# First linear map of 28 chunks by seven half-size products instead of eight

## The chip, the cores and the metric

The kernel runs on one core of one Trainium2 chip. A core has TensorE (PE, with its weight loads listed apart as PEld), VectorE (DVE), ScalarE (ACT), GpSimd (POOL) and SyncE (SP, which only issues DMAs here), each with its own in-order queue. They share the on-chip memory SBUF; TensorE writes its results to eight PSUM banks of 128 x 512 fp32, from which VectorE and ScalarE read. The metric is device time in microseconds (us) from start to end; lower is better. "The span" is the time from the first to the last instruction in one profiled execution.

## The reference

Two layers, all in fp32, on x of 8 batches x 2048 nodes x 256 features:

```python
A_norm = A + eye(n);  deg = A_norm.sum(0) + A_norm.sum(1) - diagonal(A_norm)
A_hat = A_norm * rsqrt(deg)[:, None] * rsqrt(deg)[None, :]
agg = einsum('nm,bmd->bnd', A_hat, features)            # 2048 x 2048 per batch
h   = relu(batchnorm(agg.reshape(-1, 256) @ W1.T + b1)) # first linear map, 256 -> 512
out = batchnorm(h @ W2.T + b2)                          # second linear map, 512 -> 256
x = layernorm(x + out)                                  # layer 0
x = layernorm(x + masked_attention(x, W, adj))          # layer 1, 4 heads, adj == 0 masked
```

The two batch norms take their mean and variance over all 8 x 2048 rows, so every row of h has to exist before the first relu. The change lies in `agg @ W1.T + b1`.

## The kernel before

**Stages.** (1) The adjacency matrix is loaded, transposed on TensorE into eight quarter tiles, and the degrees are summed. (2) The aggregation and the first linear map, which this document is about. (3) The last four chunks of the first linear map, then batch norm, relu and the second linear map, with h read back from HBM. (4) Attention, the longest stage.

**The aggregation** runs over 16 units `(k, b, d)`: k (0 or 1) picks two chunks of 512 output nodes, b a pair of batches, d a half (128) of the features. One unit is itself done by a seven-product scheme (Strassen-Winograd): seven products p1 to p7 instead of eight, each eight fp32 matmuls of 128x128 by 128x512 into one PSUM bank (pool `psa`, four banks). Its stationary operands are the forms `S` of x: four loaded tiles, scaled by `dinv` on GpSimd (`scale`, L303), and their sums and differences `s1` to `s4` (L316 to L328, GpSimd). Its moving operands are the quarters `T` of the adjacency matrix and their forms `t1` to `t4` (VectorE, 128x4096 elements each, L429 and L341 to L349). The products leave PSUM by one ScalarE copy (L394) and seven VectorE additions into the four tiles `ag[i, j]` (i the batch of the pair, j the chunk), each of which GpSimd then multiplies by `dbc` (L414, L436, L446, L452: c11, c21, c22, c12, in this order). The next unit's x tiles are loaded by SP (L168) after p1, scaled after p2, and s1 to s4 made behind p7 and p4. A tile name of x is reused when its product is done.

**The turn.** After unit 7 k goes from 0 to 1, and all quarters T are replaced within unit 7: SP fetches them (L353), VectorE makes a mask and t1 to t4.

**Masks.** Attention needs `adj == 0` as bytes. `mask_of` (L185) makes a quarter's mask on VectorE and SP stores it; three per k, in units 1, 2 and 3 of each k (and one at the turn).

**The first linear map.** After each odd unit (d = 1) both feature halves of four chunks are there (two batches, two chunks each), and `linear` runs for each of the four: for each of four output blocks of 128, two accumulating matmuls into a bank of `psh` (three banks), a ScalarE eviction that adds b1 (L370), VectorE `bn_stats` of the result (L371), and after the four an SP store of h to HBM (L372). That is 8 matmuls for each chunk. It is done for 7 of the 8 pairs of units, 28 chunks; the last four chunks (L588) stay on chip and are not touched by the change.

**The order of the work** on every engine in stages 2 and 3 is the order in which the code is written (`manual_schedule`), and an engine that waits holds up all that is behind it in its queue. A tile of a pool with one buffer is rewritten only when its readers are done.

**The second linear map** (L538 to L581) already works by seven products of half size: GpSimd makes the forms of h (`form`, L538, 128x1024 elements), TensorE runs each product as two matmuls into a bank (L543), ScalarE copies the first product (L551), VectorE adds the rest (L569, L570, L577, and L560 where the bias is added), and `bn_stats` follow (L557).

## Time and profile before

| what | us |
|---|---|
| median of three runs (3593.39 to 3596.04) | 3595.87 |
| the profiled execution, its own time | 3594.16 |
| its span | 3592.4 |
| TensorE busy in the span | 3545.7 (99%) |
| VectorE, ScalarE, GpSimd busy | 1989.2, 1637.4, 2265.2 |
| first-map matmuls L366 (448 records), busy | 193.4 |
| aggregation matmuls L333 (1792 records), busy | 772.1 |
| mean granted TensorE clock | 0.996 |

Every fp32 matmul of this size leaves two records in the profile: 28 chunks x 8 matmuls are the 448 records of L366. Matmuls overlap in their pipeline, so a record's duration (592 ns) is longer than the distance to the next one. In a row of the timeline the columns are start and length in us, engine, line, operation, output<-input, shape, and count of the merged instructions; in brackets stand the engine's idle time before it and what ended that.

### The profile page before, as it was taken

What the parts mean: (1) busy time and instruction counts of PE and PEld (TensorE: products, weight loads), DVE (VectorE), ACT (ScalarE), POOL (GpSimd) and SP (SyncE); (2) the same over time, 40 slices, a digit from 0 to 9 for tenths busy, and PEclk for the clock granted to TensorE, in tenths of its full rate; (3) what the DMA queues carried; (4) which work ended last, traced back from release to release, by engine and by line L of the source; (5) the groups of instructions that cost most, each with busy time, mean ns of one, the idle gap of its engine ahead of it and who ended that gap; (6) DMA issues with size and microseconds to landing.
All of it is one profiled execution on the core that took longest, in us unless ns stands there. A gap on an engine that the chain in (4) does not pass through costs nothing. (4 is left out here: it accounts for less than half of the span.)

```text
span 3592.4 us, 55051 instructions
## 1 busy us (share of the span) xinstructions
PE 3545.7 (99%) x22503; PEld 1470.5 (41%) x22503; DVE 1989.2 (55%) x2929; ACT 1637.4 (46%) x2036; POOL 2265.2 (63%) x1530
## 2 busy tenths in 40 slices
PE   8999999999999999999999999999999999999997
PEld 5444444444444443343433343433343334343332
DVE  6212141220146656766766776676676676667666
ACT  5101100110135455655665665565566566566555
POOL 3543263434237647777777777777777777777777
PEclk9999999999999999999999999999999999999999
DMA  9222232221247445666566566556566556555555
GB/s 339 68 73 88 82 135 82 76 84 45 82 167 274 160 88 101 123 136 122 114 138 121 118 136 130 112 125 140 112 124 134 118 114 147 115 115 118 118 112 114
DMA packets 197142, 440.14 MB, mean 123 GB/s; under 512 B 14080, under 2 KB 121104, under 8 KB 186384
## 3 DMA queue, kind: packets, MB, share of 16 engines
q0 software_dynamic: 64656, 239.37, 35.1%
q1 hardware_dynamic: 132048, 196.11, 15.9%
q8 instruction: 178, 2.92, 0.3%
q10 hardware_dynamic: 176, 1.06, 0.1%
q14 instruction: 84, 0.69, 0.1%
HBM read 126.62 MB, written 75.51 MB: 56 GB/s over the span
## 5 line engine op out<-in xcount | busy, mean ns | idle before, releaser
L860 ACT ACTIVATE prob<-prob 128x1024 f32<-128x1024 f32 x1024 | 1081.2, 1056 | 913.1 <-DVE prob L854 836.8
L854 DVE SCALAR_TENSOR_TENSOR prob<-mask,st 128x1024 f32<-128x1024 uint8 x1024 | 1239.1, 1215 | 434.4 <-PE st L842 358.4
L872 PE MATMUL out_ps<-prob,v 64*64 64x512 f32 x8192 | 1074.2, 595 | 3.6 <-DVE ot L898 2.6
L842 PE MATMUL st<-qt,kt 64*64 64x512 f32 x8192 | 1062.8, 589 | 0.1
L893 POOL TENSOR_TENSOR acc<-acc,prob 128x1024 f32<-128x1024 f32 x319 | 829.4, 2600 | 7.7 <-DMA prob<-prob 2.7
L333 PE MATMUL pa<-t,x 128*128 128x512 f32 x1792 | 772.1, 593 | 2.7 <-ACT x L309 2.7
L882 POOL DMA_DIRECT2D prob<-prob x447 | 403.8, 929 | 566.2 <-PE out_ps L872 456.0
L842 PEld LDWEIGHTS st<-qt,kt 64*64 64x64 f32 x8192 | 312.5, 133 | 566.7 <-issue 526.4
L333 PEld LDWEIGHTS pa<-t,x 128*128 128x128 f32 x1792 | 341.0, 190 | 431.8 <-issue 427.8
L872 PEld LDWEIGHTS out_ps<-prob,v 64*64 64x64 f32 x8192 | 290.7, 133 | 542.4 <-issue 468.0
L414 POOL TENSOR_TENSOR ag<-ag,dbc 128x512 f32<-128x512 f32 x16 | 20.2, 1264 | 484.9 <-DVE ag L413 452.3
L884 POOL TENSOR_TENSOR acc<-acc,prob 128x1024 f32<-128x1024 f32 x126 | 298.1, 2366 | 7.5
L370 ACT ACTIVATE h<-ph,b1s 128x512 f32<-128x512 f32 x112 | 76.9, 687 | 404.4 <-PE ph L366 404.4
L777 PE MATMUL pm<-x1t,wq 128*128 128x512 f32 x512 | 250.8, 613 | 0.7 <-ACT x1t L746 0.7
L394 ACT COPY ag<-pa 128x512 f32<-128x512 f32 x16 | 9.4, 586 | 421.5 <-PE pa L333 408.2
L366 PE MATMUL ph<-ag,w1s 128*128 128x512 f32 x448 | 193.4, 592 | 0.0
L891 POOL TENSOR_TENSOR acc<-prob 128x1024 f32<-128x1024 f32 x64 | 171.1, 2673 | 1.7 <-DMA prob<-prob 1.7
L672 ACT ACTIVATE x<-x,ln_nm,ln_rs 128x256 f32<-128x256 f32 x256 | 137.5, 586 | 10.5 <-POOL ln_nm L668 10.5
L777 PEld LDWEIGHTS pm<-x1t,wq 128*128 128x128 f32 x512 | 86.9, 189 | 118.3 <-issue 111.6
L944 DVE SCALAR_TENSOR_TENSOR x<-pm,ri,x 128x64 f32<-128x64 f32 x512 | 109.5, 276 | 43.8 <-PE pm L936 43.8
L371 DVE BATCH_NORM_STATS2 st<-h 128x6 f32<-128x512 f32 x112 | 76.8, 692 | 99.1 <-ACT h L370 99.1
L366 PEld LDWEIGHTS ph<-ag,w1s 128*128 128x128 f32 x448 | 85.1, 190 | 107.1 <-issue 106.9
(139 smaller groups left out, 2614.3 us busy)
## 6 DMA issues: line engine op xcount, KB each, us to landing
prob<-prob POOLq DMA_DIRECT2D x447, 512.0 KB, 4.9
x<-in_x_dram SPq DMA_DIRECT2D x92, 512.0 KB, 5.3
h_d<-h SPq DMA_DIRECT2D x28, 1024.0 KB, 3.9
t<-h_d SPq DMA_DIRECT2D x28, 1024.0 KB, 8.4
a<-in_adj_dram SPq DMA_DIRECT2D x16, 1024.0 KB, 5.0
y_d<-ag SPq DMA_DIRECT2D x32, 512.0 KB, 2.6
out_dram<-x SPq DMA_DIRECT2D x31, 512.0 KB, 6.5
yt<-y_d SPq DMA_DIRECT2D x28, 512.0 KB, 3.2
```

The source lines that it names most:

```text
L333: nc.tensor.matmul(pa, s.t[:, m, :], t[:, m, :], start=(m == 0), stop=(m == HT - 1))
L366: nc.tensor.matmul(ph, w1s[:, d, f * P : (f + 1) * P], ag[:, d, :], start=(d == 0), stop=(d == ND - 1),)
L672: nc.scalar.activation(self.t[:, i, :], self.t[:, i, :], AF.Identity, bias=self.nm[:, i : i + 1], scale=self.rs[:, i : i + 1],)
L777: nc.tensor.matmul(pm, wq[:, d, wcols], xt[:, d, cols], start=(d == 0), stop=(d == ND - 1))
L842: nc.tensor.matmul(st[r * HD : (r + 1) * HD, h, :], kt[hs, j * P + r * HD : j * P + (r + 1) * HD], qt[hs, cols], start=True, stop=True,)
L854: nc.vector.scalar_tensor_tensor(p, mask[:, j, cols][:, None, :].to_broadcast([P, 2, CH]), MASKED, st, op0=ALU.mult, op1=ALU.add,)
L860: nc.scalar.activation(probs[g], probs[g], AF.Exp)
L872: nc.tensor.matmul(outs[u][hs, r, :], inp.qkv[b, hp][2][rs, j, hs], probs[g][rs, h, :], start=(j == 0), stop=(j == NT - 1),)
L882: nc.gpsimd.dma_start(probs[g - 1], probs[g], accum_op=ALU.add)
L884: nc.gpsimd.tensor_add(accs[u], accs[u], probs[g])
L891: nc.gpsimd.tensor_add(accs[v], probs[g - 7], probs[g - 5])
L893: nc.gpsimd.tensor_add(accs[v], accs[v], probs[g - 5])
```

## The change

The first linear map of a batch i is now done for its two chunks together, by the same kind of seven-product scheme. W1 is cut in four blocks of 128 inputs x 256 outputs, the four tiles `ag[i, c][:, j, :]` (feature half j, chunk c) are the blocks of the other factor, and each of the seven products is a 128-deep product with 256 outputs: two matmuls, each alone in a PSUM bank. So 14 matmuls take the place of 16 for a batch, 28 of 32 for a pair of units.

- **Forms of W1** (`w1f`): four 128x256 additions on GpSimd, once, ahead of the first unit.
- **Forms of ag** (`linear_form`): four 128x512 subtractions on GpSimd for each batch; form 1 ahead of p7 of the odd unit, form 2 in a new tile `g2`, forms 3 and 4 within `linear`, written over operands that a product has just read.
- **Evictions**: ScalarE copies the first product (two banks); VectorE takes the twelve other banks with 14 instructions (additions, and additions with b1), and the eight `bn_stats` come at the end of `linear`.
- **Place**: `linear` of batch 1 stands where the map stood. `linear` of batch 0 is put off (`later`) to the next unit, between its p1 and p6, with its two stores of h ahead of that unit's loads of x in SP's queue.
- **At the turn** t4 (VectorE), s1 and s2 (GpSimd) of the next unit move behind `linear` of batch 1, and s3 and s4 behind that of batch 0; before, all stood in unit 7 ahead of the map.
- **Masks** move from units 1, 2, 3 of each k to units 2, 4, 6.
- `dbc` holds the two chunks of one k and is loaded again (two DMAs from ScalarE's queue) at the turn; `psh` has four banks; x of batch 0 for stage 4 is loaded into `h1`, `dbc` and `w1f`.

```diff
-        def linear(n, k, b, ag, j):
-            c = b * NCH + j * NK + k
-            h = hs[n % 2] = lp.tile([P, NH, CH], F32, name=f"h{n % 2}") if n > 1 else hs[n]
-            for f in range(NH):
-                ph = psh.tile([P, CH], F32, name="ph")
-                for d in range(ND):
-                    nc.tensor.matmul(
-                        ph, w1s[:, d, f * P : (f + 1) * P], ag[:, d, :],
-                        start=(d == 0), stop=(d == ND - 1),
-                    )
-                nc.scalar.activation(h[:, f, :], ph, AF.Identity, bias=b1s[:, f : f + 1])
-                nc.vector.bn_stats(st1[:, f, c, :], h[:, f, :])
-            nc.sync.dma_start(h_d[c], h)
+        def linear_form(ag, i, n):
+            b11, b12, b21, b22 = (ag[i, c][:, j, :] for j in range(2) for c in range(2))
...
+            x, y = {
+                1: lambda: (b12, b11),
+                2: lambda: (b22, G[i, 1]),
+                3: lambda: (G[i, 2], b11),
+                4: lambda: (b21, G[i, 2]),
+            }[n]()
+            nc.gpsimd.tensor_sub(G[i, n], x, y)
+
+        def linear(k, b, ag, i):
+            cs = [(b + i) * NCH + j * NK + k for j in range(2)]
+            lo, hi = (lp.tile([P, NH, CH], F32, name=f"h{j}") for j in range(2))
+            def products(w, t):
+                for s in range(2):
+                    ph = psh.tile([P, CH], F32, name="ph")
+                    nc.tensor.matmul(ph, W1[w][:, s * P : (s + 1) * P], t, start=True, stop=True)
+                    yield s, ph
...
+            for s, p in products((0, 0), ag[i, 0][:, 0, :]):
+                nc.scalar.copy(lo[:, 2 + s, :], p)
+            linear_form(ag, i, 3)
+            for s, p in products((0, 1), ag[i, 0][:, 1, :]):
+                plus(lo, s, p, lo[:, 2 + s, :])
+            linear_form(ag, i, 4)
+            for s, p in products(2, G[i, 2]):
+                nc.vector.tensor_add(hi[:, s, :], p, lo[:, 2 + s, :])
+            for s, p in products(3, G[i, 3]):
+                nc.vector.tensor_add(hi[:, 2 + s, :], p, hi[:, s, :])
+            for s, p in products((1, 1), G[i, 4]):
+                plus(lo, 2 + s, p, hi[:, 2 + s, :])
+            nc.sync.dma_start(h_d[cs[0]], lo)
+            for s, p in products(1, G[i, 1]):
+                plus(hi, 2 + s, p, hi[:, 2 + s, :])
+                nc.vector.tensor_add(hi[:, s, :], p, hi[:, s, :])
+            for s, p in products(4, ag[i, 1][:, 1, :]):
+                plus(hi, s, p, hi[:, s, :])
+            nc.sync.dma_start(h_d[cs[1]], hi)
+            for c, h in zip(cs, (lo, hi)):
+                for f in range(NH):
+                    nc.vector.bn_stats(st1[:, f, c, :], h[:, f, :])
...
+        nc.gpsimd.tensor_add(W1[1], W1[1, 0], W1[1, 1])
+        nc.gpsimd.tensor_sub(W1[2], W1[1], W1[0, 0])
+        nc.gpsimd.tensor_sub(W1[3], W1[0, 0], W1[1, 0])
+        nc.gpsimd.tensor_sub(W1[4], W1[0, 1], W1[2])
...
             p1 = product(S[v, 0, 0], T[k, (0, 0)])
+            for f in later:
+                f()
...
+            if d and not last:
+                for i in range(2):
+                    linear_form(ag, i, 1)
             p7 = product(S[v, 3], T[k, 3])
...
-            if not last:
+            if not (last or turn):
                 s1(w)
                 s2(w)
                 s3(w)
...
             nc.gpsimd.tensor_mul(c22, c22, dbc[0][:, 1, :])
+            if d and not last:
+                linear_form(ag, 1, 2)
...
-            if turn:
-                t4(k + 1, 3)
             n = v % (len(units) // NK)
-            if n in (1, 2, 3):
-                mask_of(k, ((0, 0), (1, 0), (1, 1))[n - 1])
+            if n in (2, 4, 6):
+                mask_of(k, ((0, 0), (1, 0), (1, 1))[n // 2 - 1])
...
-            if d == ND - 1:
-                for n, (i, j) in enumerate(CHUNKS):
-                    linear(v // ND * 4 + n, k, b + i, ag[i, j], j)
+            if d:
+                linear(k, b, ag, 1)
+                linear_form(ag, 0, 2)
+                if turn:
+                    t4(k + 1, 3)
+                    s1(w)
+                    s2(w)
+                later = [lambda k=k, b=b, ag=ag: linear(k, b, ag, 0)]
+                if turn:
+                    later += [lambda w=w: s3(w), lambda w=w: s4(w)]
```

More of the change, by code (lines that the diff above doesn't have):

```diff
@@ L282, in tile_gcn_then_masked_attention, with load_dbc @@
         name="psa", bufs=4, space=PSUM
-    ) as psa, tc.tile_pool(name="psh", bufs=3, space=PSUM) as psh, tc.tile_pool(
-        name="psd", bufs=1, space=PSUM
-    ) as psd, tc.manual_schedule(engines=ALL4):
-        hs = [lp.tile([P, NH, CH], F32, name=f"h{i}") for i in range(2)]
-        dbc = lp.tile([P, N], F32, name="dbc")
+    ) as psa, tc.tile_pool(name="psh", bufs=4, space=PSUM) as psh, tc.manual_schedule(engines=ALL4):
+        for j in range(2):
+            lp.tile([P, NH, CH], F32, name=f"h{j}")
+        w1f = lp.tile([P, 4, H // 2], F32, name="w1f")
+        dbc = []
+        def load_dbc(k):
+            dbc[:] = [lp.tile([P, 2, CH], F32, name="dbc")]
+            for j in range(2):
+                t0 = j * HT + k * TPC
+                nc.scalar.dma_start(
+                    dbc[0][:, j, :],
+                    dinv_d[t0 : t0 + TPC].rearrange("t p -> (t p)")[None, :].to_broadcast([P, CH]),
+                )
         def spread_dinv():
-            pd = psd.tile([NT, P], F32, name="pd")
+            pd = psh.tile([NT, P], F32, name="ph")
             nc.tensor.transpose(pd, dinv, ident)
@@ L295, in spread_dinv @@
             nc.scalar.dma_start(dinv_d, dt)
-            nc.scalar.dma_start(
-                dbc, dinv_d.rearrange("t p -> (t p)")[None, :].to_broadcast([P, N])
-            )
+            load_dbc(0)
         def scale(v, i, j, on_act=False):
@@ L353, in fetch @@
             nc.sync.dma_start(T[k, ij], bt_d[HALVES.index(ij)])
-        def half_cols(k, j):
-            c0 = (j * NK + k) * CH
-            return slice(c0, c0 + CH)
-        def linear(n, k, b, ag, j):
-            c = b * NCH + j * NK + k
-            h = hs[n % 2] = lp.tile([P, NH, CH], F32, name=f"h{n % 2}") if n > 1 else hs[n]
-            for f in range(NH):
-                ph = psh.tile([P, CH], F32, name="ph")
-                for d in range(ND):
-                    nc.tensor.matmul(
-                        ph, w1s[:, d, f * P : (f + 1) * P], ag[:, d, :],
-                        start=(d == 0), stop=(d == ND - 1),
-                    )
-                nc.scalar.activation(h[:, f, :], ph, AF.Identity, bias=b1s[:, f : f + 1])
-                nc.vector.bn_stats(st1[:, f, c, :], h[:, f, :])
-            nc.sync.dma_start(h_d[c], h)
+        W1 = {ij: w1s[:, ij[1], ij[0] * H // 2 : (ij[0] + 1) * H // 2] for ij in HALVES}
@@ new lines, in tile_gcn_then_masked_attention @@
+        W1.update({i + 1: w1f[:, i, :] for i in range(4)})
+        G = {}
+        def linear_form(ag, i, n):
+            b11, b12, b21, b22 = (ag[i, c][:, j, :] for j in range(2) for c in range(2))
+            if n == 2:
+                G[i, 2] = lp.tile([P, CH], F32, name="g2")
+            else:
+                G[i, n] = {1: b12, 3: b11, 4: b21}[n]
+            x, y = {
[5 more added lines that the diff above has]
+            nc.gpsimd.tensor_sub(G[i, n], x, y)
@@ new lines, in linear, with plus @@
+        def linear(k, b, ag, i):
[6 more added lines that the diff above has]
+                    yield s, ph
+            def plus(h, f, p, u):
+                nc.vector.scalar_tensor_tensor(
+                    h[:, f, :], p, b1s[:, f : f + 1], u, op0=ALU.add, op1=ALU.add
+                )
+            for s, p in products((0, 0), ag[i, 0][:, 0, :]):
[20 more added lines that the diff above has]
+                    nc.vector.bn_stats(st1[:, f, c, :], h[:, f, :])
@@ L374, in tile_gcn_then_masked_attention @@
+        later = []
         for i, j in ((0, 0), (1, 0), (1, 1), (0, 1)):
@@ L384, in tile_gcn_then_masked_attention @@
                 ag = {ij: lp.tile([P, ND, CH], F32, name=f"ag{ij[0]}{ij[1]}") for ij in HALVES}
-            lo, hi = half_cols(k, 0), half_cols(k, 1)
+            if v and units[v - 1][0] != k:
+                load_dbc(k)
             c11, c12, c21, c22 = (ag[ij][:, d, :] for ij in HALVES)
@@ L393, in tile_gcn_then_masked_attention @@
             p1 = product(S[v, 0, 0], T[k, (0, 0)])
+            for f in later:
+                f()
+            later = []
             nc.scalar.copy(u1, p1)
@@ L413, in tile_gcn_then_masked_attention @@
             nc.vector.tensor_add(c11, p2, u1)
-            nc.gpsimd.tensor_mul(c11, c11, dbc[:, lo])
+            nc.gpsimd.tensor_mul(c11, c11, dbc[0][:, 0, :])
             if first:
@@ L435, in tile_gcn_then_masked_attention @@
             nc.vector.tensor_add(c21, p4, u3)
-            nc.gpsimd.tensor_mul(c21, c21, dbc[:, lo])
+            nc.gpsimd.tensor_mul(c21, c21, dbc[0][:, 0, :])
             if turn:
@@ L441, in tile_gcn_then_masked_attention @@
                 scale(w, 0, 1)
-                s4(w)
+                if not turn:
+                    s4(w)
             p5 = product(S[v, 1], T[k, (0, 1)])
@@ L445, in tile_gcn_then_masked_attention @@
             nc.vector.tensor_add(u2, p5, u2)
-            nc.gpsimd.tensor_mul(c22, c22, dbc[:, hi])
+            nc.gpsimd.tensor_mul(c22, c22, dbc[0][:, 1, :])
+            if d and not last:
+                linear_form(ag, 1, 2)
             if turn:
@@ L451, in tile_gcn_then_masked_attention @@
             nc.vector.tensor_add(c12, p3, u2)
-            nc.gpsimd.tensor_mul(c12, c12, dbc[:, hi])
-            if turn:
-                t4(k + 1, 3)
+            nc.gpsimd.tensor_mul(c12, c12, dbc[0][:, 1, :])
             n = v % (len(units) // NK)
-            if n in (1, 2, 3):
-                mask_of(k, ((0, 0), (1, 0), (1, 1))[n - 1])
+            if n in (2, 4, 6):
+                mask_of(k, ((0, 0), (1, 0), (1, 1))[n // 2 - 1])
             if last:
                 break
-            if d == ND - 1:
-                for n, (i, j) in enumerate(CHUNKS):
-                    linear(v // ND * 4 + n, k, b + i, ag[i, j], j)
+            if d:
[8 more added lines that the diff above has]
+                    later += [lambda w=w: s3(w), lambda w=w: s4(w)]
         last4 = [(b + i) * NCH + j * NK + k for i, j in CHUNKS]
@@ L481, in tile_gcn_then_masked_attention @@
         x0 = []
-        for n, (name, size) in enumerate((("h1", [P, NH, CH]), ("dbc", [P, N]))):
-            t = lp.tile(size, F32, name=name)
-            t = t if n else t.rearrange("p a b -> p (a b)")
-            for i in range(2):
+        for name, size in (
+            ("h1", [P, NH, CH]), ("dbc", [P, 2, CH]), ("w1f", [P, 4, H // 2])
+        ):
+            t = lp.tile(size, F32, name=name).rearrange("p a b -> p (a b)")
+            for i in range(size[1] * size[2] * 2 // N):
                 tx = t[:, i * N // 2 : (i + 1) * N // 2].rearrange("p (t d) -> p t d", d=D)
```

## The prediction

> **What bounds the kernel now.** I read the page first: busy time by engine, then the costliest groups.

> ```profile
> PE 3545.7 (99%) x22503; PEld 1470.5 (41%) x22503; DVE 1989.2 (55%) x2929; ACT 1637.4 (46%) x2036; POOL 2265.2 (63%) x1530
> ...
> L370 ACT ACTIVATE h<-ph,b1s 128x512 f32<-128x512 f32 x112 | 76.9, 687 | 404.4 <-PE ph L366 404.4
> ...
> L366 PE MATMUL ph<-ag,w1s 128*128 128x512 f32 x448 | 193.4, 592 | 0.0
> ```

> TensorE sets the time, and in the first map it never waits (idle 0.0 before L366), while ScalarE waits for it. So a matmul less is time less, as long as its suppliers keep up. For the pace I take TensorE's timeline around the turn, the place with the most other work:

> ```profile
> 489.74 37.93 PE L333 MATMUL pa<-t,x 128*128 128x512 f32 x88
> 527.51 27.63 PE L366 MATMUL ph<-ag,w1s 128*128 128x512 f32 x64
> 554.97 55.53 PE L333 MATMUL pa<-t,x 128*128 128x512 f32 x129
> ```

> From start to start the 64 records of one pair's map take 554.97 - 527.51 = 27.46 us, 0.429 us a record, 0.858 us a matmul. A product p of eight matmuls takes 6.87 us.

> **What is removed.** 7 pairs x (32 - 28) = 28 matmuls x 0.858 = **24.0 us**. The rest is whether TensorE still finds its operands and banks.

> **The new map in a steady unit.** Matmuls that each close their own bank are not in this trace at this size. The nearest row is the second map, the same scheme with two matmuls to a bank; ScalarE's timeline shows its rhythm:

> ```profile
> 1078.38 0.59 ACT L551 COPY ag<-pa 128x512 f32<-128x512 f32 x1 [14.23 <-PE pa L543]
> ...
> 1090.40 0.59 ACT L551 COPY ag<-pa 128x512 f32<-128x512 f32 x1 [5.79 <-PE pa L543]
> ...
> 1102.42 0.59 ACT L551 COPY ag<-pa 128x512 f32<-128x512 f32 x1 [5.79 <-PE pa L543]
> ```

> 14 matmuls in 12.02 us: 0.859 each, no slower than the groups of eight. I take it for `linear` too: 14 x 0.858 = 12.02 us per batch.

> *Evictions.* There L560 (addition with bias) takes 745 ns, L569/L570 690. The map's 14 VectorE instructions are 8 of the first and 6 of the second, 8 x 0.745 + 6 x 0.69 = 10.1 us, in the 10.3 us that TensorE needs for the 12 banks. With four banks: product 1, with two instructions to a bank, is the tightest. Its banks are ready 9.4 and 10.3 us into the map, and VectorE frees them at about 11.1 and 12.5. They are the 11th and 12th; the last two use the banks of the 9th and 10th, freed by 8.6 and 9.5 and wanted at 10.3 and 11.2. So 1.7 us to spare. Then eight `bn_stats` at 0.61 to 0.69 (L371: five in a row took 3.05) end about 19.5 us after the map's start; the next VectorE instruction that matters comes with batch 0's third bank, 12.0 + 6.9 + 2.6 = 21.5 us after it. Behind batch 0's map they end about 0.6 us after p6 does; its addition is 0.6 us late, and p6's bank is wanted only four products on. Cost nothing.

> *Forms.* L414 gives 1.27 us for a 128x512 GpSimd instruction with nothing in its way. In an ordinary pair c12 is multiplied until 2.2 us after p3 ended (L452 starts 0.93 after L366's first matmul, 157.68 against 156.75). Forms 3 and 4 of batch 1 stand behind it: 3.5 and 4.8 us. The products that read them stand behind three and four others of 2 x 0.858: they start at 5.15 and 6.87. To spare: 1.6 and 2.1 us. Batch 0 has form 2 long before, and its form 3 waits only for its first product (1.7), so 3.2. Cost nothing. GpSimd has room: in the 48 us of an even unit (555 to 603) it was busy 20.5 us.

> *What moves.* Batch 0's map stands before p6, so VectorE's p6 addition, SP's three x loads and later steps shift with it. SP issued those loads 1.3 us after p1's start (556.30 against 554.97); now they stand behind hi's store, about 6.9 + 12.0 + 1.7 = 20.6 us after it. They land in 4 to 5 us more (median 5.3 on the page), 26, even with the 1 MB store (3.9) ahead 30; the first `scale` wants them after p2 and c11's multiplication, 6.9 + 12.0 + 13.7 + 2.8 = 35.4. Hidden, 5 us to spare; without that cover GpSimd's scaling would be late first, and it has some three products more. Masks (2.28 us, and 1.58 of small copies where the quarter is diagonal) stand behind c12's addition in units without a map, in front of nothing until p1 and p6 are over; their store holds SP less long than the third x load, which waits for p1's end anyway. `w1f` is four instructions of 0.72 us (L505, same shape), in the 32.6 us that GpSimd's first multiplication waited for `dbc`. The two dbc loads at the turn (0.35 us of issue each) stand on ScalarE's queue between the two maps' copies, where it is idle, and are wanted after p2.

> **The turn.** VectorE's and GpSimd's rows before:

> ```profile
> 507.72 2.28 DVE L185 TENSOR_SCALAR m<-t 128x4096 uint8<-128x4096 f32 x1
> 510.03 6.45 DVE L429 TENSOR_TENSOR t<-t,t 128x4096 f32<-128x4096 f32 x1
> ...
> 517.01 5.97 DVE L341 TENSOR_TENSOR t<-t,t 128x4096 f32<-128x4096 f32 x1
> ...
> ```

> ```profile
> 507.92 4.29 POOL L316 TENSOR_TENSOR x<-x,x 128x1024 f32<-128x1024 f32 x1
> 512.28 6.42 POOL L320 TENSOR_TENSOR x<-x,x 128x1024 f32<-128x1024 f32 x1
> 518.66 6.53 POOL L324 TENSOR_TENSOR x<-x,x 128x1024 f32<-128x1024 f32 x1
> 525.15 5.46 POOL L436 TENSOR_TENSOR ag<-ag,dbc 128x512 f32<-128x512 f32 x1
> ...
> ```

> GpSimd's 2.35 us became 4.3 to 6.5, VectorE's 4.42 (the same t2 in unit 0) 6.0. Read as rates, GpSimd works at about a quarter of its speed beside a t form. [...] t1 ends at 516.48, L320 ends 2.2 later; L320 ends at 518.70, t2 ends 4.3 later. By turns, the new order gives: form 1 of batch 0 to 511.1, t1 to 515.5, form 1 of batch 1 to 516.6, t2 to 521.0, c21 to 522.2, t3 and scale in either order to 528.4, c22 to 529.6, form 2 of batch 1 to 530.9, c12 to 532.1, form 3 to 533.4. The map starts at 527.5 and wants form 2 at 530.95 and form 3 at 532.7: **0.8 us** lost. After the map and its `bn_stats` t4 holds VectorE 4.4 us, to 551.5; batch 0's form 3 waits for it too, until 552.7, wanted at 552.3: **0.4 us**. [...] by rates (c21 4.2 us, form 1 twice 4, c22 and form 2 behind) I get some 2.2. I take 1.2, the bounds are 0 and 4 (t4 ahead of batch 0 in full).

> **The sum.** 3592.4 - 24.0 + 1.2 = 3569.6 for the span. The profiled run took 1.8 more than its span and the median of the runs is 1.7 above the profiled run: 3569.6 + 1.8 + 1.7 = **3573.1 us**, 22.8 less, 0.63%. A measurement of this kernel tells a change from none at about 0.2%, 7.2 us.

> **Rivals.**
> - *Suppliers late in every map.* A wait of 0.3 to 0.8 us in each of the 14 (a hand-over from TensorE to GpSimd to TensorE that costs more than the slack, or product 1's doubled evictions): 4 to 11 us, 3577 to 3584. For: VectorE has 10.1 us of work in 10.3. Against: four banks, 1.6 us of slack, and instructions that are queued start 0.60 to 0.77 apart in the second map, so the 10.1 is an upper figure. (The second map itself proves less: it has 7 banks to empty in 12 us, not 14.) Chance 0.16.
> - *The clock.* The granted clock was 1.00 in the second map's stage (1066 to 1118 us). [...] by the row, nothing. The row is the same engine with the same banks two matmuls apart, so it decides. Chance below 0.01.
> - *Slower: the form chain.* Forms 3 and 4 stand in a queue behind c12, which waits for VectorE. If GpSimd's part of each map came late by 1.7 us beyond its slack (24.0 / 14), the gain is gone; slower by 0.2% from 2.2 us, that is forms 3.8 us later than I have them, 3603. For: beside the mask L452 took 3.25 instead of 1.27. Against: that is 2 us and the masks are now elsewhere; beside evictions and `bn_stats` L538 kept 2.35. Chance 0.03.
> - *The gain doesn't arrive.* The later stages could take it back (attention's loads, 3588 to 3596). Against: between 500 and 1118 us TensorE was busy 615.9 of 618, so nothing in these stages waits for a fixed time, and attention follows them on the same full engine. Chance 0.05.

> **How the numbers follow.** The forecast has 0.75. Low end: no loss at the turn (-1.2) and the fastest run shown (-2.5): 3569.4. High end: the first rival at 0.6 us a map, 3573.1 + 8.4 = 3581.5. So 3569 to 3582. Faster by more than 7.2 us: 0.75 + 0.16 + the part of the last case that gives back less than 16.8 us, 0.94; same 0.03, slower 0.03.

> **What would show it.** Right: 392 records for the map, 12.0 us from its first to its last in each half, no idle before them but about 1 us in each half of the turn; GpSimd's forms of 1.26 us; aggregation, second map and attention unchanged. Wrong: idle time before the map's matmuls that ends on GpSimd's forms (the third rival) or on VectorE (the first), records more than 0.43 us apart, or a granted clock below 1.00 in the maps.

## The result, and the profile after

The changed kernel took 3571.06 us (median of four runs, 3570.33 to 3573.89), the kernel before 3594.7 in the same series: 23.6 us less. The ratio, estimated from the runs, is 0.9932 with a 95% interval of 0.992 to 0.9945 (the quotient of the two medians is 0.9934; 0.0002 is 0.7 us). 3573.1 had been predicted, 22.8 less than the 3595.87 of the first three runs of the kernel before.

The page of the changed kernel, busy time by engine and one of the costliest groups:

```profile
PE 3524.8 (99%) x22447; PEld 1461.9 (41%) x22447; DVE 2112.7 (59%) x3125; ACT 1575.7 (44%) x1952; POOL 2335.5 (65%) x1590
...
L399 ACT COPY h<-ph 128x512 f32<-128x512 f32 x28 | 16.4, 585 | 416.7 <-PE ph L390 416.7
```

TensorE lost 56 records (22503 to 22447), that is 28 matmuls. VectorE and GpSimd work 124 and 70 us more, ScalarE 62 less; none of that shows in the time. The changed kernel's groups by line, cut to the maps (after the bar: busy us, mean ns; then the idle time before them):

```profile
L390 PE MATMUL ph<-ag,w1f 128*128 128x512 f32 x168 | 76.8, 593 | 0.2 <-POOL ag L380 0.2
L390 PE MATMUL ph<-ag,w1s 128*128 128x512 f32 x168 | 76.7, 593 | 0.0
...
L390 PE MATMUL ph<-g,w1f 128*128 128x512 f32 x56 | 26.3, 593 | 0.0
```

168 + 168 + 56 = 392 records where there were 448, and TensorE's idle time before all of them is 0.2 us. Its timeline around the turn, the place where the kernel before was shown:

```profile
517.80 3.60 PE L390 MATMUL ph<-ag,w1s 128*128 128x512 f32 x8
521.23 1.88 PE L390 MATMUL ph<-g,w1f 128*128 128x512 f32 x4
523.36 1.99 PE L390 MATMUL ph<-ag,w1f 128*128 128x512 f32 x4 [0.25 <-POOL ag L380]
...
530.33 7.03 PE L341 MATMUL pa<-t,x 128*128 128x512 f32 x16
537.20 3.60 PE L390 MATMUL ph<-ag,w1s 128*128 128x512 f32 x8
...
549.21 89.43 PE L341 MATMUL pa<-t,x 128*128 128x512 f32 x208
```

Batch 1's map takes 530.33 - 517.80 = 12.53 us here, batch 0's, behind p1, 549.21 - 537.20 = 12.01. Every other map takes 12.02. So the stage lost 0.5 us once, at form 3 of the turn (523.36, where 522.95 would have been in step), and gained the rest: from the first map to the last four chunks (L588, now L656) 841.7 us against 865.2.

The profiled run's own span, 3571.8, is only 20.6 shorter than before; the other three runs of the changed kernel have spans of 3568.2 to 3569.0. What those 3 us are is told in the last section.

### The profile page after: what moved, and what is told of

It is laid out like the page before. It is cut to its first block, busy times and chain, and to the rows that moved or that the text cites. A ratio compares the mean times of both kernels' runs of the same rounds, so it can differ in the third digit from the quotient of the medians.

```text
span 3571.8 us, 55309 instructions
## 1 busy us (share of the span) xinstructions
PE 3524.8 (99%) x22447; PEld 1461.9 (41%) x22447; DVE 2112.7 (59%) x3125; ACT 1575.7 (44%) x1952; POOL 2335.5 (65%) x1590
## 5 line engine op out<-in xcount | busy, mean ns | idle before, releaser
L341 PE MATMUL pa<-t,x 128*128 128x512 f32 x1792 | 774.5, 594 | 2.7 <-ACT x L317 2.7
L341 PEld LDWEIGHTS pa<-t,x 128*128 128x128 f32 x1792 | 342.1, 191 | 431.9 <-issue 427.7
L399 ACT COPY h<-ph 128x512 f32<-128x512 f32 x28 | 16.4, 585 | 416.7 <-PE ph L390 416.7
L859 PE MATMUL pm<-wq,x1t 128*128 128x128 f32 x1024 | 125.1, 276 | 0.0
L859 PEld LDWEIGHTS pm<-wq,x1t 128*128 128x128 f32 x1024 | 119.4, 192 | 2.5 <-ACT x1t L814 1.7
L966 DVE TENSOR_TENSOR ot<-out_ps,ot 128x512 f32<-128x512 f32 x64 | 44.3, 692 | 124.4 <-ACT ot L965 124.4
```

Of the source, the lines that this page charges most:

```text
L341: nc.tensor.matmul(pa, s.t[:, m, :], t[:, m, :], start=(m == 0), stop=(m == HT - 1))
L859: nc.tensor.matmul(pm[:, j * P : (j + 1) * P], xt[:, d, t * P : (t + 1) * P], wq[:, d, wcols], start=(d == 0), stop=(d == ND - 1),)
```

## The experiments

A run is compared with runs of the kernel before on the same chip and in the same series; there that kernel took 3597.0 us (E1 to E4) and 3597.3 (E5 to E8), about 2.5 us more than above, and in the single runs beside E9 and E10 3598.7. So the ratios are compared: the changed kernel stands at 0.9932, and a difference of 0.001 is 3.6 us. By the intervals of the two ratios such a difference is good to some 5 to 8 us; the finer sums below are read from the profiles.

### E1: 28 matmuls more

```diff
-                    nc.tensor.matmul(ph, W1[w][:, s * P : (s + 1) * P], t, start=True, stop=True)
+                    for _ in range(2 if w == (0, 0) else 1):
+                        nc.tensor.matmul(
+                            ph, W1[w][:, s * P : (s + 1) * P], t, start=True, stop=True
+                        )
```

> The changed kernel with the two matmuls of each map's first product issued twice into the same bank (28 matmuls more, nothing else). Theory (TensorE is the only bound of the stage, the gain is 28 matmuls at 0.858 us): the whole gain is gone again, +24.0 us on the changed kernel, 3594 to 3596 us. Rival (suppliers set the pace of the maps, TensorE has slack in them): less than 12 us more, under 3583. Rival (the gain comes from the moved work and not from the count of matmuls): about 3571.

Measured: 3597.39 us, ratio 1.0000 (0.9992 to 1.0009). The 28 matmuls cost 0.0068, 24.5 us, the whole gain. TensorE's timeline in one pair of E1:

```profile
404.26 5.31 PE L391 MATMUL ph<-ag,w1s 128*128 128x512 f32 x12
...
417.99 7.03 PE L341 MATMUL pa<-t,x 128*128 128x512 f32 x16
```

The first product's group has 12 records for 8, and the map takes 13.73 us for 12.02: each added matmul is paid in full, at 0.858. The theory stands, both rivals fall.

### E2: the moves alone

The kernel before, with its map of eight products:

```diff
-            if not last:
+            if not (last or turn):
                 s1(w)
                 s2(w)
                 s3(w)
...
-                s4(w)
+                if not turn:
+                    s4(w)
...
-            if turn:
-                t4(k + 1, 3)
...
-            if n in (1, 2, 3):
-                mask_of(k, ((0, 0), (1, 0), (1, 1))[n - 1])
+            if n in (2, 4, 6):
+                mask_of(k, ((0, 0), (1, 0), (1, 1))[n // 2 - 1])
...
                     linear(v // ND * 4 + n, k, b + i, ag[i, j], j)
+                if turn:
+                    t4(k + 1, 3)
+                    for s in (s1, s2, s3, s4):
+                        s(w)
```

> The kernel before with the moves alone: masks in units 2, 4, 6, and at the turn t4 and s1 to s4 behind the map; the map itself with eight products as it was. Theory: TensorE did not wait there before (idle 0.0), so nothing changes, 3593 to 3597 us. Rival (part of the gain comes from the moved work): at least 5 us faster, under 3590.

Measured: 3596.83 us, ratio 0.9998 (0.9989 to 1.0006): no change. Its page still has L366 with 448 records and nothing to wait for:

```profile
L366 PE MATMUL ph<-ag,w1s 128*128 128x512 f32 x448 | 193.4, 592 | 0.0
```

These moves gain nothing by themselves. (E2 leaves out one: the old map was not put off by half into the next unit.) E3 to E5 ask what they are worth to the new map.

### E3: batch 0's map straight behind batch 1's

```diff
-                later = [lambda k=k, b=b, ag=ag: linear(k, b, ag, 0)]
-                if turn:
-                    later += [lambda w=w: s3(w), lambda w=w: s4(w)]
+                linear(k, b, ag, 0)
+                if turn:
+                    s3(w)
+                    s4(w)
```

> The changed kernel with batch 0's map straight behind batch 1's instead of behind p1 of the next unit (the turn's s3 and s4 behind it too). Theory: VectorE is still at batch 1's eight bn_stats (they end 18.4 us after the first map's start) when batch 0's third bank is full at 14.7, and ScalarE's first copy waits for the bn_stats of the tile it overwrites (to 16.0); banks come free late, about 1.2 and 0.9 us of idle TensorE, 2.1 us in each of 7 pairs, and some 4 us more at the turn, where t4 stands between: +15 to +22 us on the changed kernel, 3586 to 3593. Rival (the place does not matter, the four banks carry it): 3570 to 3574.

Measured: 3595.58 us, ratio 0.9996 (0.9987 to 1.0005), 0.0064 or 23 us over the changed kernel: nearly all of the gain is gone, and slightly more than the expected 15 to 22. TensorE's timeline in an ordinary pair (two rows), and then at the turn (one):

```profile
419.57 1.96 PE L390 MATMUL ph<-g,w1f 128*128 128x512 f32 x4 [1.14 <-ACT h L399]
421.93 1.95 PE L390 MATMUL ph<-ag,w1f 128*128 128x512 f32 x4 [0.41 <-DVE h L394]
...
549.88 3.67 PE L390 MATMUL ph<-ag,w1f 128*128 128x512 f32 x4 [5.66 <-DVE h L394]
```

ScalarE's row in the ordinary pair:

```profile
418.84 1.07 ACT L399 COPY h<-ph 128x512 f32<-128x512 f32 x2 [13.52 <-DVE st L419]
```

The waits stand where they were expected: ScalarE's copy waits for the `bn_stats` of the tile that it overwrites, then VectorE's first addition for the rest of them. An ordinary pair takes 26.05 us for 24.04, six pairs 12 us. At the turn t4 stands between, and 9 us are lost for the expected 4: the wait is 5.7, and the records behind it are slow (3.67 for four, where 1.88 is usual; last section). The place behind p1 is worth almost as much as the saved matmuls, because it gives VectorE 6.9 us to end its `bn_stats`.

### E4: the turn's work ahead of the map

```diff
-            if not (last or turn):
+            if not last:
                 s1(w)
                 s2(w)
                 s3(w)
...
-                if not turn:
-                    s4(w)
+                s4(w)
...
+            if turn:
+                t4(k + 1, 3)
...
-                if turn:
-                    t4(k + 1, 3)
-                    s1(w)
-                    s2(w)
                 later = [lambda k=k, b=b, ag=ag: linear(k, b, ag, 0)]
-                if turn:
-                    later += [lambda w=w: s3(w), lambda w=w: s4(w)]
```

> The changed kernel with the turn's work where it stood: s1 to s4 and t4 of the next unit inside unit 7, ahead of the map. Theory (GpSimd and VectorE take turns, one waits for the other's whole instruction): c21 is multiplied at about 10 us after the map's start instead of before it, c22 and form 2 some 7 us later; TensorE waits 8.5 us before the second product, 5 before the third and 1 before the fourth, +12 to +16 us, once, 3583 to 3587. Rival (they share the speed at about a quarter, or the wait is hidden): under 6 us, below 3577.

Measured: 3588.21 us, ratio 0.9974 (0.9962 to 0.9985), 0.0042 or 15 us over the changed kernel. VectorE's last t form (t4) and GpSimd's timeline at the turn:

```profile
519.94 5.48 DVE L357 TENSOR_TENSOR t<-t,t 128x4096 f32<-128x4096 f32 x1
```

```profile
521.10 6.52 POOL L332 TENSOR_TENSOR x<-x,x 128x1024 f32<-128x1024 f32 x1
527.58 1.26 POOL L495 TENSOR_TENSOR ag<-ag,dbc 128x512 f32<-128x512 f32 x1
```

TensorE's timeline of the same stretch:

```profile
519.13 1.88 PE L390 MATMUL ph<-ag,w1s 128*128 128x512 f32 x4
528.89 3.78 PE L390 MATMUL ph<-ag,w1s 128*128 128x512 f32 x4 [7.88 <-POOL ag L495]
535.72 3.10 PE L390 MATMUL ph<-g,w1f 128*128 128x512 f32 x4 [3.05 <-POOL g L380]
```

c21 is multiplied at 527.6, behind s1, s2 and s3, each of which waited for a whole t form (t4 ends at 525.42, s3 2.2 us later); 8.5 us after the map's start of 519.1, where some 10 had been worked out. TensorE waits 7.9 us before the second product, where 8.5 had been expected. The records behind it are slow (3.78 us for four; last section), which fills part of the next wait (3.0 for 5), so that the third product starts 13.2 us late for the expected 13.5. The rest of the 15 us is slow records too, and not the wait of 1 us that had been expected before the fourth.

Nor does the total choose between the two readings. The "under 6 us" doesn't follow from rates: from 508.1 on, beside t1, t2 and t4 (4.9, 5.3 and 5.5 us), a GpSimd at a quarter of its speed would end its three forms of 2.35 us about 1 us earlier than it did, by an estimate from these durations. What speaks for turns is the ends of the rows, here and at the turn of the changed kernel ("Why the prediction was right").

### E5 and E9: the masks where they were, and there without the small copies

```diff
-            if n in (2, 4, 6):
-                mask_of(k, ((0, 0), (1, 0), (1, 1))[n // 2 - 1])
+            if n in (1, 2, 3):
+                mask_of(k, ((0, 0), (1, 0), (1, 1))[n - 1])
```

> The changed kernel with the masks in units 1, 2, 3 of each k as before. Theory: in the four units with a map, the mask (2.28 us) and the small copies (1.58) stand ahead of the map's evictions, and c12's multiplication takes 3.25 us instead of 1.27: third bank freed at 5.45 us where 5.15 is wanted, form 3 ready at 5.5: 0.3 to 0.5 us of idle TensorE in each, 1.2 to 2 us in all, to be seen as idle time before the map's matmuls, not in the total. Rival (moving the masks carried a good part of the gain): more than 5 us of idle TensorE.

Measured (one run): 3584.91 us beside 3597.3 of the kernel before, where a ratio of 0.9932 would be 3572.8: 12 us over the changed kernel. VectorE's timeline in the first masked unit with a map:

```profile
160.17 3.75 DVE L190 COPY m<-mdiag 128x128 uint8<-128x128 uint8 x4
163.84 1.40 DVE L394 SCALAR_TENSOR_TENSOR h<-ph,b1s,h 128x512 f32<-128x512 f32 x2
```

And TensorE's row at the wait in the same map:

```profile
164.72 3.56 PE L390 MATMUL ph<-ag,w1f 128*128 128x512 f32 x4 [2.37 <-DVE h L394]
```

The expectation was wrong by its size: 2.5 us of delay in each of the four units and not 0.3 to 0.5. TensorE is idle for 9.5 us before the maps, so the rival's line of 5 us is passed: in this kernel the place of the masks carries a good part of the gain. The four small copies took 3.75 us where 1.58 was known from the kernel before. To see whether they are the reason, E9 adds one edit:

```diff
-        if i == j:
+        if False:
             for q in range(TPC):
                 m = k * TPC + q
```

> The kernel with the masks in units 1, 2, 3, with the four small copies of a diagonal quarter left out (the diagonal blocks of the mask are then made from the quarter itself, which has the identity added). Before, with the copies, TensorE waited 2.5 us in each of the four masked units with a map, where 0.3 to 0.5 had been expected; the copies took 3.75 us instead of 1.58. Theory (each small copy and each form of GpSimd wait for one another in turn, and so the copies hold up the evictions): without the copies VectorE is free 3.1 us after the map's start and the third bank at 3.9, before it is wanted; what is left is form 3 behind c12, ready at 5.5 where 5.15 is wanted: 0.2 to 0.5 us of idle TensorE in each of the four, 2 us at most in all. Rival (the mask itself holds the map up): still 1.5 us or more in each.

Measured (one run): 3576.33 us, where the kernel before took 3598.7 beside it, 22.4 less and so about the changed kernel's gain; with one run of each, the rows below carry the reading and not this difference. VectorE's timeline in the same unit of E9:

```profile
160.21 1.46 DVE L394 SCALAR_TENSOR_TENSOR h<-ph,b1s,h 128x512 f32<-128x512 f32 x2
```

TensorE's row at the place of the wait:

```profile
162.71 1.99 PE L390 MATMUL ph<-ag,w1f 128*128 128x512 f32 x4 [0.19 <-POOL ag L380]
```

Without the copies VectorE comes to the evictions 3.8 us earlier (3.0 us after the map's start, 157.21, for 6.8), and 0.2 us of wait is left, on form 3. So it was the copies. A summary of them in the kernel before and in E5 (ns, min/median/max):

```profile
L189 DVE COPY m<-mdiag x16: 215/217/1174, 159.8 to 779.2; 128x128 uint8<-128x128 uint8 x16
L190 DVE COPY m<-mdiag x16: 212/1234/1301, 160.2 to 776.1; 128x128 uint8<-128x128 uint8 x16
```

A copy with nothing in its way takes 0.21 to 0.22 us. Before, only the first of four was long; in E5 three of four are. In the unit shown they take 1.17, 1.30, 1.30 and 0.21 us, and the three long ones end at 161.34, 162.56 and 163.78, each 0.08 us after an instruction of GpSimd (c12, form 3, form 4). Each of the three waited for a whole instruction, and two such waits more are the 2.2 us by which the time grew.

### E6: form 3 later by 3 us

```diff
+            if i:
+                for _ in range(4):
+                    nc.gpsimd.tensor_sub(W1[3], W1[0, 0], W1[1, 0])
             linear_form(ag, i, 3)
```

> The changed kernel with GpSimd making one form of W1 again four times (4 x 0.72 = 2.9 us) ahead of form 3 of batch 1 in every pair; the values stay the same. Theory (form 3 is ready 1.6 us before its product, no more): TensorE waits 1.3 us in each of six pairs and about 2.9 more at the turn, +10.7 us, 3580 to 3584. Rival (the forms have much more room than 1.6 us): within 2 us of the changed kernel. Rival (forms and evictions together stall more than by this sum): over 3588.

Measured: 3588.76 us, ratio 0.9976 (0.9967 to 0.9986), 0.0044 or 16 us over the changed kernel; 10.7 had been expected. (3588.76 is just past the line of "stalls more than by this sum", but only by the 2.5 us by which this series is slower.) TensorE in an ordinary pair and at the turn:

```profile
407.15 1.98 PE L390 MATMUL ph<-ag,w1f 128*128 128x512 f32 x4 [1.30 <-POOL ag L380]
...
530.91 3.78 PE L390 MATMUL ph<-ag,w1f 128*128 128x512 f32 x4 [3.33 <-POOL ag L380]
...
537.29 3.60 PE L390 MATMUL ph<-ag,w1f 128*128 128x512 f32 x8
```

In the ordinary pair form 3's product starts 1.45 us late, behind four repeats that took 3.1 us: the slack is 1.65 us, 1.6 was predicted. Six such pairs are 8.7 us. Most of the surplus is at the turn: 3.1 us of additional wait, about as expected, and then eight records take 6.38 us from the first start to the start of the next group (530.91 to 537.29), where 3.54 is usual.

### E7 and E8: two and three banks

```diff
-    ) as psa, tc.tile_pool(name="psh", bufs=4, space=PSUM) as psh, tc.manual_schedule(engines=ALL4):
+    ) as psa, tc.tile_pool(name="psh", bufs=2, space=PSUM) as psh, tc.manual_schedule(engines=ALL4):
```

E8 is the same edit with `bufs=3`.

> The changed kernel with two PSUM banks for the map instead of four. Theory: a bank's turn is matmul 0.86, hand-over 0.1, eviction 0.69, hand-over 0.1 us, 1.75 against the 1.72 that two matmuls take, and product 1 with two instructions to a bank costs about 1 us: 1 to 2 us in each of 14 maps, 3585 to 3599. Rival (TensorE's own pace hides it): 3570 to 3574.

> The changed kernel with three banks for the map. Theory: only the last matmul touches a limit (it wants the bank freed 10.99 us after the map's start at 11.16 us), so 0 to 0.1 us in each map, 3570 to 3574. Rival (four banks are needed): more than 0.4 us in each of the 14 maps, over 3577.

Measured: two banks 3609.93 us, ratio 1.0033 (1.0021 to 1.0045), 36 us over the changed kernel, beyond the expected range and slower than the one before; three banks 3574.67, ratio 0.9936 (0.9919 to 0.9952), no difference that can be told from the changed kernel. A map with two banks:

```profile
412.79 1.96 PE L390 MATMUL ph<-ag,w1f 128*128 128x512 f32 x4
414.76 1.96 PE L390 MATMUL ph<-ag,w1s 128*128 128x512 f32 x4
416.70 1.99 PE L390 MATMUL ph<-ag,w1f 128*128 128x512 f32 x4
419.27 2.38 PE L390 MATMUL ph<-ag,w1f 128*128 128x512 f32 x4 [0.58 <-DVE h L413]
```

A product takes 1.97 us for 1.72, and product 1 2.57. Two banks mean that the cycle of matmul (0.86), eviction (0.69) and the hand-overs sets the pace; it is 1.97, so by the difference of these durations the two hand-overs are about 0.4 us together, where 0.2 was the author's estimate. A map takes 14.5 us. With the third bank they are hidden: TensorE's idle time before the maps of E8 is 0.2 us, as in the changed kernel. The fourth has no measurable part in the gain.

### E10: waits of several lengths

E3, E4, E5 and E6 had slow records behind waits. E10 puts waits of chosen length into the six pairs away from the turn:

```diff
+        LATE = {1: 5, 3: 6, 5: 7, 7: 0, 9: 8, 11: 10, 13: 14}
...
+            for _ in range(LATE[v] if i else 0):
+                nc.gpsimd.tensor_sub(W1[3], W1[0, 0], W1[1, 0])
             linear_form(ag, i, 3)
```

> The changed kernel with one form of W1 made again by GpSimd ahead of form 3 of batch 1, 5, 6, 7, 8, 10 and 14 times in the pairs other than the turn's: TensorE waits about 0.78 us for each less 1.7, so 2.2, 3.0, 3.8, 4.5, 6.1 and 9.2 us. In the earlier runs the granted clock fell to 0.5 behind waits of 2.4 (once of two), 3.3, 5.7 and 7.9 us. Theory (the clock is a matter of the wait's length): behind waits of 3.8 us and more the clock is 0.5 for 3 to 6 us each time, so each of these costs 1.7 to 3 us beyond itself, behind 2.2 and 3.0 sometimes; 3608 to 3618 us in all. Rival (the slow records belong to the turn or to single runs): no record above its usual distance outside the waits, 3600 to 3605 us.

Measured (one run): 3612.53 us. TensorE's first records behind five of the six waits (the wait of 6.1 us is like that of 4.5):

```profile
165.16 3.50 PE L390 MATMUL ph<-ag,w1f 128*128 128x512 f32 x4 [2.11 <-POOL ag L380]
...
290.20 1.98 PE L390 MATMUL ph<-ag,w1f 128*128 128x512 f32 x4 [2.91 <-POOL ag L380]
...
414.34 3.51 PE L390 MATMUL ph<-ag,w1f 128*128 128x512 f32 x4 [3.71 <-POOL ag L380]
...
661.67 3.78 PE L390 MATMUL ph<-ag,w1f 128*128 128x512 f32 x4 [4.51 <-POOL ag L380]
...
923.69 3.44 PE L390 MATMUL ph<-ag,w1f 128*128 128x512 f32 x4 [9.33 <-POOL ag L380]
```

Behind all but one the next four records took 3.4 to 3.8 us where 1.98 is usual behind a short wait. The table of stretches around the wait of 4.5 us has the granted clock in its column PEclk (third last; the first columns are the stretch and its length):

```profile
661.70:665.20 3.50, 3.50 (x4) 1.48 (x5) 0.69 (x1) 0.00 (x0) 2.41 (x2) 0.50 0.00 0
...
668.00:671.30 3.30, 3.30 (x9) 1.48 (x8) 3.03 (x5) 0.00 (x0) 0.00 (x0) 1.00 0.48 199
```

So the clock is the cause of the slow records, and they belong neither to the turn nor to single runs.

## Why the prediction was right

**The total: right, and closer than it could claim.** The median came within 2 us of 3573.1, while the runs themselves lie between 3570.33 and 3573.89. What the profile carries is the sum by stage.

**The removed matmuls: right.** 24.0 us for 28 matmuls. The stage became 23.5 us shorter with 0.5 lost at the turn, and E1 gives the price from the other side, 24.5 us for 28 more.

**The steady unit at no cost: right**, in every term that can be seen. Map 12.02 us, no idle time. Form 3's slack 1.65 us (E6) for 1.6. `bn_stats` ended 18.3 us after the map's start for 19.5. SP issued the x loads 20.9 us after p1's start for 20.6. The banks never held a map up, and three are already enough (E8).

**The turn: right in its mechanism, too high in its size.** 0.5 us instead of 1.2. The first term, form 3 behind the t forms, was 0.5 for 0.8. The reading by turns (the one instruction waits for the whole of the other) can be checked in the rows of the changed kernel, VectorE's t1 and GpSimd's c21:

```profile
506.22 4.89 DVE L349 TENSOR_TENSOR t<-t,t 128x4096 f32<-128x4096 f32 x1
506.79 5.45 POOL L495 TENSOR_TENSOR ag<-ag,dbc 128x512 f32<-128x512 f32 x1
```

t1 ends at 511.11 and c21 at 512.24, so nearly the whole of its 1.26 us lies behind t1. By rates it was to take 4.2 us; it took 5.45.

The second term, batch 0's form 3 behind t4, was 0.4 and came to nothing. VectorE's and GpSimd's rows at that place:

```profile
536.55 4.40 DVE L357 TENSOR_TENSOR t<-t,t 128x4096 f32<-128x4096 f32 x1
540.88 1.40 DVE L394 SCALAR_TENSOR_TENSOR h<-ph,b1s,h 128x512 f32<-128x512 f32 x2
```

```profile
539.16 2.92 POOL L380 TENSOR_TENSOR ag<-g,ag 128x512 f32<-128x512 f32 x1 [8.53 <-PE ph L390]
```

Form 3 does wait for t4, but t4 ends 3.7 us after that map's start (537.20), where the sum had some 4.3, and form 3 is ready at 542.08, 0.3 us before its product (542.35). The sum is also not consistent: with its own 19.5 us for the `bn_stats` and the 0.8 of the first term t4 would end at 552.2, not 551.5, and the term be 1.1. The `bn_stats` ended earlier than 19.5, and so the smaller figure was the better one.

**Work that was costed at nothing because it is covered: right, but its cover was worth more than I had it.** The text said of the masks only that nothing waits for them in their new place. E5 shows what the old place would have cost, 2.5 us in each of four units, and E3 that the place of batch 0's map carries about 23 us, nearly all of the gain. By E2 the moves of the masks and of the turn's work are worth nothing to the old map. The gain is the matmuls; the moves are what lets it arrive.

**The rivals.** Suppliers late in every map did not happen; two banks (E7) show what it would have looked like. A wait of 0.3 us or more in a map appears only in the variants. The clock fell in no map of the changed kernel (it was 1.00 from 63.8 to 1224.3 us, and the maps end before 1000), as the row of the second map had said; the new map has hardly any gaps (0.2 us in all). In E7, with about 0.25 us lost at each product, the map shown has no slow records either (1.95 to 2.38 us for four). Longer gaps were another matter: behind some of the waits of 2.1 us and more in E3 to E6 and E10 the clock fell to about 0.5 (last section). That would have belonged to the price of the third rival: in E10 a wait of 2.1 us in a map cost 1.7 us more. The later stages took back nothing but 2 us at the start of attention, in the profiled run (last section).

## What to carry to other kernels

On a full TensorE a matmul less is worth its distance to the next one (0.858 us here), and the scheme with seven products gives it only if each product's bank and each form arrives in step; list for every product who frees its bank and who makes its operand, with the slack, and look for what stands ahead of them in their queues. Here the `bn_stats` (4.8 us) in front of the evictions were enough to lose nearly all of the gain, a mask with its copies (6 us) half of it, and a place behind some unrelated product (6.9 us) was enough to keep it. Where instructions of GpSimd and VectorE are seen to take turns, add them up one after the other, small ones too: here the t forms (c21's 1.26 us became 5.45 beside t1), the mask (c12's became 3.24 in E5) and its copies (0.21 us became up to 1.30) against GpSimd's forms and multiplications. Additions out of PSUM and `bn_stats` did not take turns with them (GpSimd's forms kept 1.27 us beside the one in the changed kernel, 2.36 beside the other in the second map before).

## What the runs showed of the hardware that was not expected

A wait of TensorE can cost more than its length. Behind the waits of 3.7, 4.5, 6.1 and 9.3 us in E10 the next eight records took 5.0 to 6.5 us from the first start to the start of the next group, where 3.54 is usual, so 1.5 to 3 us more were lost each time; behind the wait of 4.5 us the granted clock was 0.50. At 2.1 us 1.7 were lost in the same way, at 2.9 us nothing. Of two waits in E5 that were nearly equal, that of 2.37 us had a clock of 0.52 behind it, and that of 2.36 us one of 1.00.

```profile
162.07:165.48 3.41, 1.30 (x4) 1.00 0.00 0
165.48:168.89 3.41, 3.41 (x5) 0.50 0.00 0
...
284.95:288.36 3.41, 2.34 (x6) 1.00 0.00 0
288.36:291.77 3.41, 1.57 (x4) 1.00 0.00 0
291.77:295.18 3.41, 3.41 (x9) 1.00 0.00 0
```

The wait of 2.11 us lies in one stretch of the grid, and the next stretch has half the clock. The longer one is split in 1.07 and 1.84 us and costs nothing. So 2.11 us of idle TensorE in a stretch were enough here, and 1.84 were not. The traces of the two kernels agree, from 60 to 3500 us, counted with the starts and ends that the profile gives the records: the clock fell after two stretches, with 3.41 us of idle TensorE before and 2.48 after, and after none of some 2,000 others at full clock, which had at most 1.47; it came back after a stretch with 0.59 us in the kernel before and after one with none in the changed kernel, where one with 0.67 had not been enough.

The kernel itself has such a place, at the start of attention, where TensorE waits 5.9 us. TensorE's row a few matmuls later, in the kernel before:

```profile
1263.61 3.70 PE L777 MATMUL pm<-x1t,wq 128*128 128x512 f32 x8 [0.68 <-ACT x1t L746]
```

The same in the changed kernel:

```profile
1240.56 5.78 PE L845 MATMUL pm<-x1t,wq 128*128 128x512 f32 x8 [0.67 <-ACT x1t L814]
```

The same eight records took 2.1 us more in the profiled run of the changed kernel; the granted clock over them was 0.63, and 1.00 before. In the same way the first product of unit 0, behind a wait of 2.7 us in both kernels, took 9.7 us for 8.5 at 0.72 against 0.82. Together that accounts for the 3 us by which the span of this run had shrunk less than those of the others, whose mean granted clock was 0.995 or 0.996 for its 0.994. The waits at both places are the same in the two kernels (5.9 and 2.7 us), so it is no effect of the saved matmuls, but of where the grid fell. At the start of attention the grid cut the wait of the kernel before in 1.47, 3.41 and 1.01 us, and half clock lasted from 1249.75 to 1263.40, just ahead of the row shown; it cut that of the changed kernel in 2.48 and 3.41, so that half clock came one stretch earlier against the work, and lasted from 1224.29 to 1244.77, into the row shown.
